# One transformer block on one core: transfers beside the weights issued by rank and spaced apart, gets in four parts

## The chip, the core and the metric

The kernel runs on one core of a Trainium2 chip. The metric is the device time of one execution in microseconds (us). Three runs of the kernel before took 3470.78 to 3471.49 us, median 3471.28 us. One more execution was recorded by the hardware profiler; all views below are of that one.

## What is computed

The input `x` has 8 sequences of 1024 rows of 512 numbers, `cond` one row of 512 per sequence; everything is float32. Per sequence (cut to what matters):

```python
mod = silu(condition) @ Wada + bada
sh_a, sc_a, gt_a, sh_m, sc_m, gt_m = split(mod, 6, axis=1)
xm = layernorm(x, g1, be1) * (1 + sc_a) + sh_a
x  = x + gt_a * attention(xm, Wqkv, Wproj, bproj)   # causal, 16 heads of 32
xm = layernorm(x, g2, be2) * (1 + sc_m) + sh_m
x  = x + gt_m * (gelu(xm @ W1 + b1) @ W2 + b2)      # W1 512x2048
```

## The kernel before

**Tiling.** The 8 x 1024 rows are cut into 16 blocks of 512 (`blocks`, numbered `n`, two per sequence). Each 512x512x512 product is done by a Strassen-like scheme of seven products of 256x256x256 (`strassen`); such a product is 32 matmul records of the profile, and its weights are one piece `w` of 256 KB. Sums of weight quarters are made once and kept in HBM (`kept_up_S`, `kept_down_S`, `kept_qkv_S`, `kept_proj_S`).

**Order of the work.** The program is one straight list of instructions for each engine, written by a planner inside the kernel. It keeps an estimated clock per engine (`now`), the time at which each value will be there (`written`), and two streams on TensorE: attention (`attend`), and the linear steps listed by window in `plan` (line 277 to 313). Of several threads it takes the one whose operands are due first (`work`, `step_aside`). A value whose transfer has not been issued stands at `NEVER`. In window `w`, with `n = w - 1`, from the third window on the steps are: the last "up" steps of block `n - 1`; the load of the residual rows of block `n` (`load_xr`); `v` of block `w`; the output projection of `n` (`proj`); its second normalization (`mt`); the "down" steps of `n - 1`; `q` and `k` of block `w + 1`; the first "up" steps of `n`, among them the load of the rows of a later block (`load_xa`).

**Transfers.** Nearly all are issued by SyncE (queue SP), in the order in which the planner emits them, and each waits there for what it needs:
- Weight pieces go through a ring of 9 buffers (`fetch`, line 380): a piece is fetched when the one nine places ahead has been used. Each fetch moves `queue_free`, the planner's idea of the queue, on by 450 ns.
- Rows of `x` for the first normalization (`load_x`, line 426, into the one buffer `hat`) and residual rows (`load_xr`, line 1442, into `xr`) are four transfers of 256 KB each, emitted together on the spot.
- From block 4 on for the first normalization (key `a`) and from block 3 to 13 for the second (key `m`), rows are turned by way of HBM instead of on TensorE (`turn_rows`, line 758): DVE transposes 32x32 squares, four puts of 256 KB (line 776) write them to `turned`, and one get of 1 MB (line 782) reads them back as `xm`. Then `modulated` scales each of the four column blocks `c` of `xm` (line 841 or 847). The first "up" product needs `c` = 0 and 1 only; the operands of most later ones need all four.
- Results are stored per half block (`store`, line 1266): two transfers of 256 KB at once.
- Puts, gets and stores stand in the list `transfers`; `run_transfers` (line 630) emits the one with the earliest ready time once `queue_free` and that time have passed, and moves `queue_free` on by 700 ns. A get becomes ready 7000 ns after the last put. `run_transfers(True)` empties the list at once; `stored_by` calls it when a buffer is to be reused whose stores are not yet emitted.
- Rows of the gates are broadcast from HBM (`gate_broadcasts`, line 595), two of 256 KB for the attention gate, on the spot; for even `n` this stands right before `load_xr`.

Of the kernel before, what the change touches and what calls it, by code (L numbers as in the profile page):

```python
# [22 lines left out]
def kernel(  # L23
# [261 lines left out]
    for w in range(1, NB):  # L285
        n = w - 1
        m = mlp_steps(n)
        even = blocks[n][1] == 0
        rows_a = [("rows", blocks[n][0], "a")] if even else []
        rows_m = [("rows", blocks[n][0], "m")] if even else []  # L290
        at = [("at", w + 2)] if w + 2 < NB else []
        ups = m[:1] + ([("load_xa", w + 2)] if w + 2 < NB else []) + m[1:3]
        ups += ([("norm_a", w + 2)] if w + 2 < NB else []) + m[3:4] + at
        head = rows_a + [("load_xr", n)]
        if w == 1:
            steps = head + [("k", w + 1), ("proj", n), ("mt", n), ("q", w + 1)]
# [12 lines left out]
        if w == NB - 1:  # L309
            plan[w] += late + downs[:2]  # L310
            downs = downs[2:]
# [111 lines left out]
    def row_tile(name):  # L423
        return tmp.tile([P, NTT, D], F32, tag="hat", name=name, bufs=1)

    def load_x(n):
        b, h = blocks[n]
        rows = row_tile(f"hat_{n}")
        if is_turned(f"a{n}"):
            for a in range(P // SQ):  # L430
                r0 = h * TB + a * P
                nc.sync.dma_start(
                    rows[a * SQ : (a + 1) * SQ, :, :],
                    x[b, r0 : r0 + P, :].rearrange("(t r) d -> r t d", r=SQ),
                )
        else:
            for t in range(NTT):
                nc.sync.dma_start(rows[:, t, :], x[b, h * TB + t * P : h * TB + (t + 1) * P, :])
        return [rows[:, t, :] for t in range(NTT)]

    x_pre = {0: load_x(0)}
    ada = {}
    for i in (1, 0):
        ada[i] = act.tile([P, NC, TB], F32, tag="hT", name=f"ada_{i}", bufs=NQ)
# [180 lines left out]
                return  # L625
            jobs.pop(i)[0]()

    transfers = []

    def run_transfers(everything=False):  # L630
        while transfers:
            i = min(range(len(transfers)), key=lambda i: transfers[i][0])
            if not everything and max(queue_free[0], transfers[i][0]) > now["PE"]:
                return
            ready, transfer = transfers.pop(i)
            queue_free[0] = max(queue_free[0], now["PE"], ready) + 700
            transfer()

    pool_jobs = []
# [33 lines left out]
    def normalize(tiles, key, sources):  # L673

        for t in range(NTT):
            written["hat", key, t] = NEVER
        mv = small.tile([P, NTT, 2], F32, tag="mv", name=f"mv_{key}")
        rstd = small.tile([P, NTT], F32, tag="rstd", name=f"rstd_{key}")
        offset = small.tile([P, NTT], F32, tag="offset", name=f"offset_{key}")
        got = []  # L680

        def statistics(t):
            st = small.tile([P, nc.vector.BN_STATS_DIM], F32, tag="st", name=f"st_{key}_{t}")
# [64 lines left out]
    def turn_first():  # L748
# [6 lines left out]
                note_pe(TR, "whole", [("hat", "a0", t)], ["st"])  # L755
        first_turned.append(st)

    def turn_rows(key, tiles, xm):

        squares = xm.rearrange("p c (j r) -> p (c j) r", r=P)  # L760
# [2 lines left out]
        def turn(t):  # L763
# [4 lines left out]
            if t == NTT - 1:  # L768
                ready = now["DVE"] + SYNC
                for a in range(P // SQ):  # L770
                    transfers.append((ready, lambda a=a: put(a)))

        def put(a):
            if a == P // SQ - 1:
                transfers.append((queue_free[0] + 7000, get))
            nc.sync.dma_start(
                there[:, ts(a, P)].rearrange("(k r) n -> r k n", r=SQ),
                squares[a * SQ : (a + 1) * SQ, :, :],
            )

        def get():
            nc.sync.dma_start(xm, there.rearrange("(c p) n -> p c n", p=P))
            written["spread", key] = queue_free[0] + 5000

        written["spread", key] = NEVER
        for t in range(NTT):
            add_job(lambda t=t: turn(t), [("hat", key, t)], key)

    def modulated(key, gain, shift, b, guards):
# [26 lines left out]
        turned = first_turned.pop() if key == "a0" else None  # L816
        if rows_turned:
            turn_rows(key, got, xm)
            yield [("spread", key)], []
        for c in range(NC):  # L820
            if rows_turned:
                if c:
                    yield [("spread", key)], []
                from_ps, held = xm[:, c, :], ("spread", key)
            elif turned is None:
                if c:
                    yield [("hat", key, 0)], [BANK]
# [308 lines left out]
    def project_half(n):  # L1136
# [3 lines left out]
        for other in ("B11", "B21", "B22"):  # L1140
            written[f"p{n}", other] = written["att", n]
        for t in range(NTT):
            xt_job = lambda t=t: add_to(
                residual[n][:, t, :], gate_rows["gba"], [("row", "gba")], [("xr", n, t)]
            )
            pool_jobs.append((xt_job, [("xr", n, t)]))
# [1 line left out]
        def put(f, t, bank, ps, other, reads, last):  # L1148
# [7 lines left out]
            else:  # L1156
                combine_out(y, bank, ps, other, reads, [ky], last=last)
                add_to(y, gate, [("row", "ga")], [ky], ALU.mult)
            add_to(residual[n][:, half(t, 2), c], y, [ky], [("xr", n, 2 * t), ("xr", n, 2 * t + 1)])

        def done():
            run_pool_jobs(True)
            normalize([residual[n][:, t, :] for t in range(NTT)], f"m{n}", [("xr", n, t) for t in range(NTT)])
            written["normal", n] = 0.0
# [4 lines left out]
    def project_out(n):  # L1169
# [2 lines left out]
        attT = qTs[n]  # L1172
        tiles = [residual[n][:, t, :] for t in range(NTT)]
        for t, xt in enumerate(tiles):
            xt_job = lambda t=t, xt=xt: add_to(xt, gate_rows["gba"], [("row", "gba")], [("xr", n, t)])
            pool_jobs.append((xt_job, [("xr", n, t)]))
        last = n == NB - 1
        begun = []
# [87 lines left out]
    def store(n, t):  # L1266
# [4 lines left out]
        unstored.append(n)  # L1271

        def move():
            unstored.remove(n)
            for i in (2 * t, 2 * t + 1):
                nc.sync.dma_start(rows[i], residual[n][:, i, :])

        transfers.append((ready + 1000, move))

    def stored_by(n):  # L1280
        while n in unstored:
# [136 lines left out]
    def perform(step):  # L1418
# [7 lines left out]
        elif kind == "gates":  # L1426
            yield from gates(step[1])
        elif kind == "load_xa":
            x_pre[step[1]] = load_x(step[1])
            written["x", f"a{step[1]}"] = now["PE"] + 6000  # L1430
        elif kind == "load_xr":
            n = step[1]
            b, h = blocks[n]
# [5 lines left out]
            else:  # L1439
                xr = xrp.tile([P, NTT, D], F32, tag="xr", name=f"xr_{n}")  # L1440
            residual[n] = xr
            for t, rows in enumerate(row_tiles_of(x[b, h * TB : (h + 1) * TB, :], n)):
                nc.sync.dma_start(xr[:, t, :], rows)
# [652 lines left out]
```

## Time and profile before

| | |
|---|---|
| median of 3 runs | 3471.28 us |
| the profiled execution | 3470.92 us |
| its span, first to last instruction | 3469.2 us |
| TensorE weight load, busy | 1778.0 us (51%) |
| VectorE busy | 2055.4 us (59%) |
| ScalarE busy | 1301.4 us (38%) |
| GpSimd busy | 1944.2 us (56%) |
| moved by DMA | 489.91 MB, mean 141 GB/s |

The engines are PE (TensorE), PEld (its weight loads), DVE (VectorE), ACT (ScalarE), POOL (GpSimd) and SP (SyncE, which issues transfers). A row of the list of waits reads: engine, line, what it waited for: total us, times, longest. A row of the timeline reads: start, length, engine, line, operation, out<-in, count, and in brackets how long the engine had been idle and what ended that. A piece of the chain of waits reads: start, length, what. A row of the table by stage reads: stretch, length, then busy us (and instructions) of PE, PEld, DVE, ACT and POOL, the granted TensorE clock, the busy share of the DMA engines, and GB/s.

### The profile page before, as it was taken

The numbers are of one execution on the slowest core, as the hardware profiler recorded it, in microseconds if no ns is written. First come the engines' busy times: TensorE is split into PE (matmuls) and PEld (weight loads), VectorE is DVE, ScalarE is ACT, GpSimd is POOL, SyncE is SP. The second block draws the span as 40 slices with busy tenths as digits, with TensorE's granted clock in tenths as the row PEclk, the third lists the DMA queues.
The fourth block names the chain that finished last, engine by engine and source line by source line (L and its number), as shares of the span: only waits on it lengthen the run. The fifth ranks groups of instructions, "written<-read, shape, count | busy, mean of one in ns | idle before, by whom it ended". The sixth has DMA issues, their size and how long they took to land.

```text
span 3469.2 us, 122474 instructions
## 1 busy us (share of the span) xinstructions
PE 3423.4 (99%) x55442; PEld 1778.0 (51%) x55442; DVE 2055.4 (59%) x2262; ACT 1301.4 (38%) x1444; POOL 1944.2 (56%) x2101
## 2 busy tenths in 40 slices
PE   8999999999999999999999999999999999999999
PEld 5544554555545554455554555454554545544555
DVE  6765666646565465664756547575466745656364
ACT  2345244343343433434333353443524334242421
POOL 3766757656267471774626755277553774446530
PEclk9999999999999999999999999999999999999999
DMA  6833434345544454444544445444464454633444
GB/s 226 277 127 87 120 108 138 109 117 159 156 141 134 127 152 146 138 136 128 167 135 144 136 132 175 127 140 135 133 187 121 129 150 121 187 115 88 120 143 136
DMA packets 378508, 489.91 MB, mean 141 GB/s; under 512 B 27284, under 2 KB 234444, under 8 KB 377988
## 3 DMA queue, kind: packets, MB, share of 16 engines
q1 hardware_dynamic: 377792, 481.79, 47.1%
q8 instruction: 437, 7.16, 0.9%
q14 instruction: 83, 0.68, 0.1%
q10 hardware_dynamic: 196, 0.28, 0.0%
HBM read 428.44 MB, written 53.53 MB: 139 GB/s over the span
## 4 chain that ended last, share of the span: by engine, by line
PE 89%; DVE 4%; DMA 4%; ACT 1%; issue 1%; POOL 1%; SPq 0%; DVEq 0%; ACTq 0%; POOLq 0%
PE bank L233 62%; PE sc L1692 8%; PE po L1826 7%; PE st L1785 7%; PE st L1773 3%; DVE mx L1709 2%; DMA w<-kept_proj_S 2%; PE bank L1847 2%; DMA w<-in_L_cond_Wproj_dram 1%; DVE sc L1706 1%; ACT pT L1798 1%; DMA xm_m<-turned_m 1%; PE bank L1747 0%; DVE hT L1299 0%; DMA xr<-in_x_dram 0%
## 5 line engine op out<-in xcount | busy, mean ns | idle before, releaser
L1911 POOL TENSOR_TENSOR pT<-pT,pT 128x256 f32<-128x256 f32 (+3 forms) x1254 | 1213.5, 1003 | 143.1 <-ACT pT L1798 112.3
L1798 ACT ACTIVATE pT<-st 128x2048 f32<-128x2048 f32 x288 | 541.1, 1879 | 1075.2 <-PE st L1785 989.3
L233 PE MATMUL bank<-w,hT 128*32 128x256 f32 x14336 | 814.1, 380 | 0.0
L1709 DVE TENSOR_REDUCE mx<-sc 128x4 f32<-128x2048 f32 (+3 forms) x384 | 665.7, 1754 | 215.3 <-PE sc L1692 209.2
L233 PEld LDWEIGHTS bank<-w,hT 128*32 128x32 f32 x14336 | 454.5, 110 | 357.6 <-issue 74.7
L233 PE MATMUL bank<-xm_m,w 128*32 128x256 f32 x8192 | 500.7, 381 | 4.6 <-DVE xm_m L841 4.5
L1803 POOL TENSOR_SCALAR_AFFINE_SELECT pT<-pT 128x512 f32<-128x512 f32 x256 | 177.1, 710 | 436.8 <-ACT pT L1798 431.5
L233 PE MATMUL bank<-t_m,w 128*32 128x256 f32 x6144 | 384.2, 381 | 0.1
L233 PEld LDWEIGHTS bank<-xm_m,w 128*32 128x32 f32 x8192 | 257.2, 110 | 228.7 <-issue 65.1
L1692 PE MATMUL sc<-kT,qT 32*128 32x512 f32 (+3 forms) x3072 | 329.3, 520 | 2.9 <-DVE mx L1709 1.8
L1706 DVE TENSOR_TENSOR sc<-sc,mask 128x1024 f32<-128x1024 f32 (+1 forms) x160 | 162.8, 1017 | 242.9 <-PE sc L1692 167.2
L1826 PE MATMUL po<-pT,v 128*32 128x512 f32 (+3 forms) x3072 | 304.9, 491 | 0.0
L1785 PE MATMUL st<-qT,kT 32*128 32x512 f32 (+3 forms) x3072 | 300.1, 486 | 0.0
L233 PEld LDWEIGHTS bank<-t_m,w 128*32 128x32 f32 x6144 | 190.2, 110 | 178.4 <-issue 51.7
L233 PE MATMUL bank<-xm_a,w 128*32 128x256 f32 x3968 | 239.3, 380 | 2.4 <-ACT xm_a L847 1.1
L190 POOL TENSOR_TENSOR qT<-top,rec 128x512 f32<-128x512 f32 x60 | 78.5, 1309 | 276.1 <-ACT rec L1865 276.1
L222 DVE TENSOR_TENSOR hT<-bank,u_u 128x512 f32<-128x512 f32 x192 | 130.0, 686 | 153.2 <-PE bank L233 150.7
L1692 PEld LDWEIGHTS sc<-kT,qT 32*128 32x128 f32 x3072 | 129.7, 184 | 161.5 <-issue 54.7
L233 PE MATMUL bank<-w,qT 128*32 128x256 f32 (+1 forms) x2944 | 191.6, 399 | 3.2 <-DMA w<-in_L_cond_Wproj_dram 3.2
L233 PE MATMUL bank<-t_a,w 128*32 128x256 f32 x2944 | 181.7, 380 | 0.0
L233 PEld LDWEIGHTS bank<-xm_a,w 128*32 128x32 f32 x3968 | 127.7, 110 | 97.4 <-issue 13.9
L1230 ACT ACTIVATE hT<-hT,cols 128x512 f32<-128x512 f32 x256 | 164.2, 711 | 27.2 <-DVE hT L222 26.5
(240 smaller groups left out, 3418.2 us busy)
## 6 DMA issues: line engine op xcount, KB each, us to landing
w<-in_L_cond_W_dram SPq DMA_DIRECT2D x384, 256.0 KB
w<-kept_up_S SPq DMA_DIRECT2D x256, 256.0 KB
w<-kept_down_S SPq DMA_DIRECT2D x256, 256.0 KB
w<-kept_qkv_S SPq DMA_DIRECT2D x180, 256.0 KB
w<-in_L_cond_Wqkv_dram SPq DMA_DIRECT2D x147, 256.0 KB
hat<-in_x_dram SPq DMA_DIRECT2D x64, 256.0 KB
xr<-in_x_dram SPq DMA_DIRECT2D x64, 256.0 KB
out_dram<-xr SPq DMA_DIRECT2D x64, 256.0 KB
```

Of the source, the lines that this page charges most:

```text
L222: nc.vector.tensor_tensor(out, src, other, op)
L233: nc.tensor.matmul(ps[r], columns, rhs, start=start, stop=stop, skip_group_check=True)
L1230: nc.scalar.activation(hT[:, i, :], hT[:, i, :], AF.Gelu, bias=cols[:, O_B1 + f : O_B1 + f + 1])
L1692: nc.tensor.matmul(sc[:, j, c0 : c0 + w], qTs[n][r, gg, ts(qt, P)], keys_of(n, kh)[r, gg, :w], start=True, stop=True, skip_group_check=True,)
L1706: nc.vector.tensor_tensor(place, place, shape_of.to_broadcast(place.shape), ALU.add)
L1709: nc.vector.tensor_reduce(maxima[n, gg][:, kh, qt, :], sc[:, :, c0 : c0 + w], axis=AX.X, op=ALU.max)
L1773: nc.tensor.matmul(st[:, j, c0 : c0 + w], minus_ones[r, :], row[r, TB - w :], start=(c0 == 0), stop=False, skip_group_check=True,)
L1785: nc.tensor.matmul(st[:, j, c0 : c0 + w], kT[r, gg, ts(k % NTT, P)], qT[r, gg, TB - w :], start=False, stop=True, skip_group_check=True,)
L1798: nc.scalar.activation(pT[:, :, :used], st[:, :, :used], AF.Exp, scale=scale)
L1803: nc.gpsimd.affine_select(diagonal, diagonal, pattern=[[0, HPG], [1, P]], compare_op=ALU.is_ge, fill=0.0, base=0, channel_multiplier=-1,)
L1826: nc.tensor.matmul(po[r, TB - w :], v[:, k % NTT, g * P + j * hd : g * P + (j + 1) * hd], pT[:, j, c0 : c0 + w], start=(k == 0), stop=last ...
L1911: nc.gpsimd.tensor_tensor(into, into, pT[:, j, c0 : c0 + w], ALU.add)
```

## The change

Every transfer but a weight, a kept sum and a gate row now goes through `transfers` with a rank: PATH (puts and gets) before LOAD (rows) before STORE. Of those that are ready, the lowest rank goes first, and each moves `queue_free` on by 1700 ns. Rows are loaded in four entries of their own, a store is two entries, and the get is four of 256 KB, one per `c`, each with its own time of arrival. Before a use of rows whose load has not been emitted, `arrived` empties the list. The assumed times of arrival change. The attention gate's rows of the next sequence move from before `load_xr` of an even block to the end of the window before, ahead of the first "up" step.

```diff
-        rows_a = [("rows", blocks[n][0], "a")] if even else []
+        rows_a = [("rows", blocks[n][0], "a")] if n == 0 else []
...
-        plan[w] = steps + rows_m + ups[:i]
+        rows_a = [("rows", blocks[w][0], "a")] if not even else []
+        plan[w] = steps + rows_m + rows_a + ups[:i]
...
-    transfers = []
+    transfers, coming = [], []
+
+    PATH, LOAD, STORE = range(3)
+    SPACE = 1700
...
         while transfers:
-            i = min(range(len(transfers)), key=lambda i: transfers[i][0])
-            if not everything and max(queue_free[0], transfers[i][0]) > now["PE"]:
+            due_now = [i for i, (ready, *_) in enumerate(transfers) if ready <= now["PE"]]
+            if everything:
+                i = min(range(len(transfers)), key=lambda i: transfers[i][0])
+            elif queue_free[0] > now["PE"] or not due_now:
                 return
-            ready, transfer = transfers.pop(i)
-            queue_free[0] = max(queue_free[0], now["PE"], ready) + 700
+            else:
+                i = min(due_now, key=lambda i: transfers[i][1::-1])
+            ready, _, transfer = transfers.pop(i)
+            queue_free[0] = max(queue_free[0], now["PE"], ready) + SPACE
             transfer()
...
+    LANDED = 5500
...
         def put(a):
             if a == P // SQ - 1:
-                transfers.append((queue_free[0] + 7000, get))
+                for c in range(NC):
+                    transfers.append((queue_free[0] + LANDED, PATH, lambda c=c: get(c)))
...
-        def get():
-            nc.sync.dma_start(xm, there.rearrange("(c p) n -> p c n", p=P))
-            written["spread", key] = queue_free[0] + 5000
-
-        written["spread", key] = NEVER
+        def get(c):
+            nc.sync.dma_start(xm[:, c, :], there[ts(c, P), :])
+            written["spread", key, c] = queue_free[0] + 3000
+
+        for c in range(NC):
+            written["spread", key, c] = NEVER
...
+    def arrived(what):
+        while what in coming:
+            run_transfers(True)
+
...
-    LANDING = 10000
+    LANDING = 6000
...
-        transfers.append((ready + 1000, move))
+        for i in (2 * t, 2 * t + 1):
+            unstored.append(n)
+            transfers.append((ready + 1000, STORE, lambda i=i: move(i)))
...
-            x_pre[step[1]] = load_x(step[1])
-            written["x", f"a{step[1]}"] = now["PE"] + 6000
+            def later(load):
+                coming.append(key)
+                transfers.append((now["PE"], LOAD, lambda: landing(load)))
+
+            def landing(load):
+                load()
+                coming.remove(key)
+                written[key] = NEVER if key in coming else queue_free[0] + 4000
...
+            def load(t, rows):
+                coming.remove(("xr", n))
+                nc.sync.dma_start(xr[:, t, :], rows)
+                written["xr", n, t] = max(now["PE"], stored.get(n - 1, 0.0), queue_free[0]) + LANDING
+
             for t, rows in enumerate(row_tiles_of(x[b, h * TB : (h + 1) * TB, :], n)):
-                nc.sync.dma_start(xr[:, t, :], rows)
-                landed = max(now["PE"], stored.get(n - 1, 0.0)) + LANDING + 700 * t
-                written["xr", n, t] = landed
+                written["xr", n, t] = NEVER
+                coming.append(("xr", n))
+                transfers.append((now["PE"], LOAD, lambda t=t, rows=rows: load(t, rows)))
```

More of the change, by code (lines that the diff above doesn't have):

```diff
@@ L424, in row_tile, with load_x @@
         return tmp.tile([P, NTT, D], F32, tag="hat", name=name, bufs=1)
-    def load_x(n):
+    def load_x(n, later):
         b, h = blocks[n]
         rows = row_tile(f"hat_{n}")
+        pairs = []
         if is_turned(f"a{n}"):
@@ L431, in load_x @@
                 r0 = h * TB + a * P
[L432 to L435, printed above, removed]
+                from_x = x[b, r0 : r0 + P, :].rearrange("(t r) d -> r t d", r=SQ)
+                pairs.append((rows[a * SQ : (a + 1) * SQ, :, :], from_x))
         else:
             for t in range(NTT):
-                nc.sync.dma_start(rows[:, t, :], x[b, h * TB + t * P : h * TB + (t + 1) * P, :])
+                r0 = h * TB + t * P
+                pairs.append((rows[:, t, :], x[b, r0 : r0 + P, :]))
+        for to, from_x in pairs:
+            later(lambda to=to, from_x=from_x: nc.sync.dma_start(to, from_x))
         return [rows[:, t, :] for t in range(NTT)]
-    x_pre = {0: load_x(0)}
+    x_pre = {0: load_x(0, lambda load: load())}
     ada = {}
@@ L682, in statistics @@
         def statistics(t):
+            arrived(("x", key))
             st = small.tile([P, nc.vector.BN_STATS_DIM], F32, tag="st", name=f"st_{key}_{t}")
@@ L770, in turn @@
                 for a in range(P // SQ):
-                    transfers.append((ready, lambda a=a: put(a)))
+                    transfers.append((ready, PATH, lambda a=a: put(a)))
         def put(a):
             if a == P // SQ - 1:
-                transfers.append((queue_free[0] + 7000, get))
+                for c in range(NC):
+                    transfers.append((queue_free[0] + LANDED, PATH, lambda c=c: get(c)))
             nc.sync.dma_start(
@@ L822, in modulated @@
                 if c:
[L823 to L824 removed]
+                    yield [("spread", key, c)], []
+                from_ps, held = xm[:, c, :], ("spread", key, c)
             elif turned is None:
@@ L1158, in put @@
                 add_to(y, gate, [("row", "ga")], [ky], ALU.mult)
+            arrived(("xr", n))
             add_to(residual[n][:, half(t, 2), c], y, [ky], [("xr", n, 2 * t), ("xr", n, 2 * t + 1)])
         def done():
+            arrived(("xr", n))
             run_pool_jobs(True)
@@ L1174, in project_out @@
         for t, xt in enumerate(tiles):
-            xt_job = lambda t=t, xt=xt: add_to(xt, gate_rows["gba"], [("row", "gba")], [("xr", n, t)])
+            xt_job = lambda t=t, xt=xt: arrived(("xr", n)) or add_to(xt, gate_rows["gba"], [("row", "gba")], [("xr", n, t)])
             pool_jobs.append((xt_job, [("xr", n, t)]))
@@ L1270, in store, with move @@
         stored[n + 1] = max(stored.get(n + 1, 0.0), ready)
-        unstored.append(n)
-        def move():
+        def move(i):
             unstored.remove(n)
-            for i in (2 * t, 2 * t + 1):
-                nc.sync.dma_start(rows[i], residual[n][:, i, :])
-        transfers.append((ready + 1000, move))
+            nc.sync.dma_start(rows[i], residual[n][:, i, :])
+        for i in (2 * t, 2 * t + 1):
+            unstored.append(n)
+            transfers.append((ready + 1000, STORE, lambda i=i: move(i)))
     def stored_by(n):
@@ L1428, in perform @@
         elif kind == "load_xa":
-            x_pre[step[1]] = load_x(step[1])
-            written["x", f"a{step[1]}"] = now["PE"] + 6000
+            key = ("x", f"a{step[1]}")
+            def later(load):
[5 more added lines that the diff above has]
+                written[key] = NEVER if key in coming else queue_free[0] + 4000
+            written[key] = NEVER
+            x_pre[step[1]] = load_x(step[1], later)
         elif kind == "load_xr":
```

4 lines of the change are left out of this document (2 added, 2 removed).

## The prediction, made before the changed kernel had run

> **What bounds the kernel now.** I read the page's first part first, for the share of each engine, and then the list of what TensorE waited for, which says how much a change of transfers could give at all.
>
> ```profile
> span 3469.2 us, 122474 instructions
> ...
> PE 3423.4 (99%) x55442; PEld 1778.0 (51%) x55442; DVE 2055.4 (59%) x2262; ACT 1301.4 (38%) x1444; POOL 1944.2 (56%) x2101
> ```
>
> PE is busy for all but 3469.2 - 3423.4 = 45.8 us. The change leaves every matmul in place, so whatever it gains has to come out of these 45.8 us, apart from matmuls that ran slowly. The list of waits of PE over the whole span names the pieces:
>
> ```profile
> PE st L1773 <- DVE mx L1709: 7.5, 12, 1.9
> PE bank L1747 <- POOL mcols L1731: 5.9, 7, 1.6
> PE bank L520 <- DMA ada<-in_L_cond_Wada_dram: 5.3, 1, 5.3
> PE bank L233 <- DVE xm_m L841: 4.5, 1, 4.5
> ...
> PE bank L233 <- DMA w<-in_L_cond_Wproj_dram: 3.2, 2, 1.6
> PE bank L233 <- DMA w<-kept_proj_S: 2.3, 4, 0.8
> ```
>
> The largest two, 13.4 us, are the softmax maxima on DVE and POOL, which the change does not touch. The 5.3 us are the first load of the program, also untouched. Within reach are three rows: 3.2 + 2.3 = **5.5 us** of waiting for weights of the output projection, six times, and **4.5 us** of one wait for the turned rows of a block.
>
> **Term 1: the weights of the projection.** The timeline of SP and the chain of waits show the longest of the six, at block 6:
>
> ```profile
> 1406.09 0.47 SPq L599 DMA_DIRECT2D row_ga<-kept_ga  x1
> 1406.61 0.42 SPq L599 DMA_DIRECT2D row_gba<-kept_gba  x1
> 1407.08 3.03 SPq L1443 DMA_DIRECT2D xr<-in_x_dram  x4
> 1410.21 4.48 SPq L390 DMA_DIRECT2D w<-in_L_cond_Wproj_dram  x2
> ```
>
> ```profile
> 1410.21 15.27 DMA w<-in_L_cond_Wproj_dram
> ```
>
> ```profile
> 1425.62 1.50 PE L233 MATMUL bank<-w,qT 128*32 128x256 f32 x24 [1.65 <-DMA w<-in_L_cond_Wproj_dram]
> ```
>
> Six transfers of 256 KB leave SP in 4 us, the first projection weight stands behind them, needs 15.27 us to land, and the matmul comes 1.65 us too early. How fast such a burst drains is seen at block 5, where POOL uses the residual rows tile by tile:
>
> ```profile
> 1202.27 2.53 SPq L1443 DMA_DIRECT2D xr<-in_x_dram  x4
> ```
>
> ```profile
> 1208.24 1.29 POOL L190 TENSOR_TENSOR xr<-xr,row_gba 128x512 f32<-128x512 f32 x1 [14.33 <-DMA xr<-in_x_dram]
> 1212.01 1.28 POOL L190 TENSOR_TENSOR xr<-xr,row_gba 128x512 f32<-128x512 f32 x1 [2.48 <-DMA xr<-in_x_dram]
> 1215.80 1.26 POOL L190 TENSOR_TENSOR xr<-xr,row_gba 128x512 f32<-128x512 f32 x1 [2.51 <-DMA xr<-in_x_dram]
> ```
>
> Beside the weights a tile lands every 3.8 us. When SP has issued four in 2.53 us, about 4 - 2.53/3.8 = 3.3 stand ahead of the next weight. After the change they are emitted at least 1700 ns apart, and with a weight's 450 ns between them 2.15 us; when the fourth is out, 6.45 us have passed and 4 - 6.45/3.8 = 2.3 are left. So the worst weight has one tile less ahead of it, up to 3.8 us, against a longest wait of 1.65 us; at even blocks the two gate rows are gone from this place as well. I take all of **-5.5 us**. The other end is 0, should only the place of the burst move. The gate rows now stand ahead of the first up step, with no burst of rows behind them; I cost them at nothing, since weights there have the same nine-piece lead, and at 1.65 us each if that cover is gone.
>
> **Term 2: the turned rows of block 5.** SP's timeline, the chain, and PE's timeline:
>
> ```profile
> 1294.32 0.43 SPq L776 DMA_DIRECT2D turned_m<-xm_m  x1
> ...
> 1299.40 0.76 SPq L776 DMA_DIRECT2D turned_m<-xm_m  x1
> 1300.26 1.97 SPq L1276 DMA_DIRECT2D out_dram<-xr  x2
> ...
> 1304.55 2.15 SPq L1276 DMA_DIRECT2D out_dram<-xr  x2
> ...
> 1310.71 1.18 SPq L782 DMA_DIRECT2D xm_m<-turned_m  x1
> ```
>
> ```profile
> 1310.71 11.04 DMA xm_m<-turned_m
> ```
>
> ```profile
> 1316.04 1.91 PE L233 MATMUL bank<-t_a,w 128*32 128x256 f32 x32
> 1322.43 3.51 PE L233 MATMUL bank<-xm_m,w 128*32 128x256 f32 x32 [4.48 <-DVE xm_m L841]
> 1326.15 1.93 PE L233 MATMUL bank<-xm_a,w 128*32 128x256 f32 x32 [0.21 <-DVE u_k L222]
> ```
>
> ```profile
> 1319.00:1324.00 5.00, 1.57 (x17) 0.94 (x21) 2.15 (x4) 0.82 (x1) 0.00 (x0) 0.86 0.59 215
> ```
>
> Four stores are issued right after the puts; the get follows 11.3 us after the last put and takes 11.04 us. PE idles 4.48 us, and the granted clock of that stretch is 0.86: the product behind the gap takes 3.51 us where its like takes 1.91 us. So the wait costs 4.48 + 1.60 = 6.1 us, more than its row in the list. [...]
>
> After the change the first parts become ready 1700 + 5500 = 7.2 us after the last put was emitted, against 700 + 7000 = 7.7 us; the puts themselves, 1.7 us apart in the trace, come 2.15 us apart, so the last one up to 1.35 us later. The four parts start at least 1.7, more often 2.15 us apart: the last starts 5.1 to 6.45 us after the first. Part 1 thus starts 1.2 to 3.0 us later than the whole get would have, but lands without the other half ahead of it; half of 11.04 us is 5.5 us. The first up product needs parts 0 and 1 only: it gains 5.5 - 1.2 = 4.3 us at best and 2.5 us at worst. The other products need part 3, which starts 4.6 to 7.3 us later than the get did; its own quarter, 2.8 us, replaces 11.04 us, so it lands between 3.6 us earlier and 1.0 us later. The tail of `k` (two products, the first at 1326.15, some 3.5 us) stands ready to fill the space in between, which the planner now sees, since it knows each part's own arrival. I take **-4 us** out of 6.1. The ends: -6.1 if nothing is waited for any more, and +6 if the parts come as late as they are emitted and land no faster.
>
> Elsewhere the turned rows have time to spare; block 7, on SP, ACT and PE:
>
> ```profile
> 1724.59 0.39 SPq L782 DMA_DIRECT2D xm_m<-turned_m  x1
> ```
>
> ```profile
> 1730.32 2.93 ACT L847 ACTIVATE xm_m<-xm_m,shiftm,gainm 128x512 f32<-128x512 f32 x4 [16.60 <-DMA xm_m<-turned_m]
> ```
>
> ```profile
> 1756.20 1.94 PE L233 MATMUL bank<-xm_m,w 128*32 128x256 f32 x32
> ```
>
> They land 5.7 us after the get and are used 25.9 us after that. A chain 6 us longer is hidden there by the `q` and `k` products.
>
> **What costs nothing, and why.** Three more issues for each of the 23 gets (`a` of blocks 4 to 15, `m` of 3 to 13) are 69 x 0.39 us (the get of block 7, above) = 27 us of SP, which is far from the bound:
>
> ```profile
> SPq L392 <- PE bank L233: 1436.5, 682, 21.8
> ...
> SPq L390 <- DMA xr<-in_x_dram: 41.3, 18, 3.3
> ```
>
> SP waits 1436.5 us for PE to free weight buffers in one row alone. The 41.3 us, fetches held up behind bursts of rows, should shrink. Without that cover the 27 us would show in weights that land late. Rows and stores that come some us later are hidden as long as their users have the `v` step or more ahead of them; the residual rows' first use lies behind the seven products of `v`, 13 us at 1.91 us each, and four entries at 2.15 us take 8.6 us. Only in window 2 does the projection follow the load directly; there the list may be emptied once. Should `arrived` or `stored_by` empty the list, SP gets a burst like those of before, at the price that they have now, up to 1.65 us each. At the end of the program the issue order decides the last half microsecond:
>
> ```profile
> 3463.65 0.36 SPq L1356 DMA_DIRECT2D out_dram<-xr  x1
> 3464.06 1.37 SPq L1276 DMA_DIRECT2D out_dram<-xr  x2
> 3466.12 0.33 SPq L1356 DMA_DIRECT2D out_dram<-xr  x1
> ```
>
> If the second of the two L1276 stores slips behind the last L1356, the end comes some 0.5 us later: I take +0.3, between 0 and +0.5.
>
> The planner's new times also shift the interleaving of attention and linear work everywhere. The trace cannot show that order. I bound it by the softmax waits, 7.5 + 5.9 = 13.4 us: a third more or less of these is 4 us on either side, and I take 0.
>
> **Sum.** -5.5 - 4.0 + 0.3 = -9.2 us. The profiled execution took 3470.92 us (1.7 us around its span), 0.36 us under the median of the runs; from the median, 3471.28 - 9.2 = 3462.1, rounded to **3462.0 us** (-0.27%).
>
> **Rivals.**
> 1. *Only the projection's waits go; block 5 stays as it is.* For it: 1300 to 1311 is where stores, puts and get of one block crowd, and a list emptied by `stored_by` there would send them together again. Against it: the stores have lower rank. 3471.28 - 5.5 = 3465.8 us.
> 2. *It does not do what it says for PE.* Rows, weights and stores are as many bytes as before, a spaced burst still drains at one tile per 3.8 us, and 2.15 us is faster than that; if the weights land just as late, the 5.5 us stay, block 5 stays, and the new order gives or takes up to 4 us: 3471 us, between 3467 and 3475.
> 3. *Slower: the longer way of the turned rows becomes the wait at the first up step.* The last part is emitted up to 7.3 us later. Place: the first up products of the 11 blocks from 3 to 13. Price: where no slack is left, up to 7.3 us of idling plus 1.6 us of slow clock, 8.9 us for each block. It decides once two blocks lose it, 17.8 - 5.5 = +12.3 us: 3483.6 us. Against it stand 25.9 us of slack at block 7; for it, that block 5 had none, and that the new order may move others there. [...] No row here shows a turned get in parts; the weights of 256 KB are what the trace has, and there the queue keeps many in flight.
> 4. *More than the sum.* If POOL and DVE wait less for rows, part of the 13.4 us goes too: another 5 us, 3457 us.
>
> **Chances.** The forecast 0.42 (3459 to 3465), rival 1 0.21, rival 2 0.14, rival 3 0.16, rival 4 0.07. A difference under 0.2%, 6.9 us, is about what a measurement of this kernel can tell from no change; the bound is 3464.3 us below and 3478.2 us above. Faster by more: rival 4, and the forecast but for its upper edge, 0.07 + 0.42 = 0.49, and 0.02 of rival 1, makes 0.51. Slower by more: rival 3, 0.16. Within: the rest, 0.33. The range runs from 3457 us (rival 4's middle) to 3474 us (rival 2's upper part); outside are rival 3 and half of rival 4, 0.195 in all.
>
> **What would show it.** Term 1: no wait of PE for `kept_proj_S` or `Wproj` in the list of waits, four separate `xr` issues on SP, and under 15.27 us for that weight in the chain. Term 2: no gap of 4.48 us ahead of an up step, a granted clock of 1.00 in that stretch, and the four parts of the get landing one after the other. Wrong would be a new row of waits for `xm_m` or `xm_a` at several blocks, waits for weights elsewhere in the list, or a PE busy time that differs from 3423.4 us by more than 4 us, since then it is the order of the matmuls that decides.

## The result and the profile after

The kernel after took 3463.89 us, median of 14 runs (3462.82 to 3465.78); the kernel before, on the same chip, 3471.11 us, median of 14. The ratio is 0.998, 95% interval 0.9973 to 0.9987: **7.2 us or 0.21% faster**, between 4.5 and 9.4 us. The forecast was 3462.0 us.

The profiled execution of after took 3465.39 us, 1.5 us above that median. The first part of its page:

```profile
span 3463.7 us, 122539 instructions
...
PE 3424.3 (99%) x55442; PEld 1776.1 (51%) x55442; DVE 2069.1 (60%) x2295; ACT 1288.6 (37%) x1422; POOL 1940.4 (56%) x2090
```

TensorE is idle for 3463.7 - 3424.3 = 39.4 us, where it was 45.8: 6.4 us less. The list of its waits (engine, line, what it waited for: total us, times, longest):

```profile
PE st L1812 <- DVE mx L1748: 7.5, 12, 1.9
PE bank L1786 <- POOL mcols L1770: 5.9, 7, 1.6
...
PE sc L1731 <- DVE mx L1748: 3.0, 4, 2.0
```

No row of the list names `Wproj` or `kept_proj_S` any more: the 5.5 us of Term 1 are gone as waits. The row of 4.5 us for `xm_m` is gone too (0.4 us are left), but one has grown: score units wait for the softmax maximum 3.0 us, 2.0 of them at one place, where the list of before has

```profile
PE sc L1692 <- DVE mx L1709: 1.8, 5, 0.6
```

The two softmax rows that the forecast left untouched, 7.5 and 5.9 us, are the same to a tenth of a microsecond.

The table by stage says where. Of before (stretch, length, then busy us and instructions of PE, PEld, DVE, ACT and POOL, clock, DMA share, GB/s):

```profile
25.00:100.00 75.00, 72.77 (x1189) 42.06 (x1185) 55.41 (x72) 23.04 (x31) 27.67 (x36) 1.00 0.63 205
...
1300.00:1340.00 40.00, 35.31 (x576) 18.86 (x568) 16.84 (x21) 5.08 (x7) 2.48 (x2) 0.96 0.60 190
1340.00:2000.00 660.00, 655.17 (x10571) 334.96 (x10564) 401.62 (x428) 256.98 (x280) 392.60 (x417) 1.00 0.48 138
```

The same stretches of after:

```profile
25.00:100.00 75.00, 72.76 (x1157) 41.89 (x1152) 53.80 (x71) 22.94 (x31) 25.96 (x35) 0.98 0.62 199
...
1300.00:1340.00 40.00, 36.93 (x621) 19.72 (x616) 16.62 (x20) 8.40 (x12) 5.49 (x5) 1.00 0.68 205
1340.00:2000.00 660.00, 658.48 (x10636) 336.08 (x10632) 411.41 (x443) 252.97 (x272) 393.89 (x414) 1.00 0.48 139
```

Around block 5 (1300 to 1340) idling fell from 4.69 to 3.07 us and the clock rose to 1.00, and from 1340 to 2000 it fell from 4.83 to 1.52 us. The first row shows a trap: at equal busy time, after did 32 matmuls fewer at a clock of 0.98. From 24.90 to 28.20 us its clock was 0.50; that is about 1.7 us lost near the start. It belongs to this execution and not to the change: the profiled executions of e5 and e11 below, with the matmuls in the order of after, did 1187 and 1188 in that stretch at a clock of 1.00, and that of e8, in the order of before, 1160 at 0.98. The slow stretch near the start took the place of the slow product at block 5, so PE's busy time did not fall; it also fits that this execution lies above its median.

**The projection.** SP's timeline of after at block 6:

```profile
1403.43 0.60 SPq L1478 DMA_DIRECT2D xr<-in_x_dram  x1
1404.72 0.39 SPq L391 DMA_DIRECT2D w<-in_L_cond_Wproj_dram  x1
1405.16 0.59 SPq L1478 DMA_DIRECT2D xr<-in_x_dram  x1
```

The four `xr` loads alternate with the weights, and no gate rows stand ahead of them.

**Block 5.** SP, the chain of waits, and PE:

```profile
1305.87 0.60 SPq L1296 DMA_DIRECT2D out_dram<-xr  x1
1309.35 0.58 SPq L1296 DMA_DIRECT2D out_dram<-xr  x1
1311.11 1.16 SPq L1296 DMA_DIRECT2D out_dram<-xr  x2
1312.32 4.30 SPq L796 DMA_DIRECT2D xm_m<-turned_m  x4
```

```profile
1312.32 11.26 DMA xm_m<-turned_m
```

```profile
1320.75 1.91 PE L233 MATMUL bank<-t_a,w 128*32 128x256 f32 x32
1322.59 1.14 PE L1731 MATMUL sc<-kT,qT 32*128 32x512 f32 x8
1324.41 0.64 PE L233 MATMUL bank<-xm_m,w 128*32 128x256 f32 x8 [0.68 <-issue]
1325.42 1.50 PE L233 MATMUL bank<-xm_m,w 128*32 128x256 f32 x24 [0.37 <-DVE xm_m L856]
1328.95 1.14 PE L1731 MATMUL sc<-kT,qT 32*128 32x512 f32 x8 [2.03 <-DVE mx L1748]
```

The four parts did not go out apart from each other. `stored_by`, called for `k` of block 7, emptied the list: two stores and then all four parts at once. The first part landed 11.26 us after its issue, where the whole get of before had taken 11.04 us. What did change is PE's row: the tail of `k` and a score unit now stand *ahead* of the first up product. The waits are 0.68 + 0.37 + 2.03 = 3.1 us at full clock, in place of 4.48 + 0.21 us and a product slower by 1.60 us, 6.3 us together: **3.2 us less** in this execution.

The full clock there is not certain. A later profiled execution of the same kernel (after_again, with e9 below) has nearly the same waits, 0.90 + 0.37 + 2.02 us, and then a slow product:

```profile
1329.68 1.14 PE L1731 MATMUL sc<-kT,qT 32*128 32x512 f32 x8 [2.02 <-DVE mx L1748]
1330.75 3.44 PE L233 MATMUL bank<-t_m,w 128*32 128x256 f32 x32
```

It takes 3.44 us in place of 1.93, so with 0.2 us more of waiting about half of the 3.2 us is lost again in that execution.

### The profile page after: what moved, and what is told of

Same layout as the page of the kernel before. It is cut to its first block, busy times and chain, and to the rows that moved or that the text cites. A ratio compares the mean times of both kernels' runs of the same rounds, so it can differ in the third digit from the quotient of the medians.

```text
span 3463.7 us, 122539 instructions
## 1 busy us (share of the span) xinstructions
PE 3424.3 (99%) x55442; PEld 1776.1 (51%) x55442; DVE 2069.1 (60%) x2295; ACT 1288.6 (37%) x1422; POOL 1940.4 (56%) x2090
## 4 chain that ended last, share of the span: by engine, by line
PE 90%; DVE 4%; ACT 2%; DMA 2%; issue 1%; POOL 1%; SPq 0%; DVEq 0%; ACTq 0%; POOLq 0%
PE bank L233 62%; PE sc L1731 8%; PE po L1865 7%; PE st L1824 7%; PE st L1812 3%; DVE mx L1748 2%; PE bank L1886 2%; ACT pT L1837 1%; DMA w<-kept_up_S 1%; DVE sc L1745 1%; DMA xm_m<-turned_m 1%; PE bank L1786 1%; DVE hT L1321 0%; ACT hT L1252 0%; PE bank L847 0%
```

## The experiments

The question was which of the change's parts does this. Theory A: at block 5 it is the order of the matmuls, which the planner chose because its estimate of the arrival is a later one, and at the projection it is the burst that is gone. Theory B, the forecast's: the transfers themselves, by rank, spacing and parts, land sooner. Each kernel was timed beside the kernel before on the same chip; differences are against that.

**e1: the order alone.** In the kernel before, one number: the arrival that the planner assumes for the second rows of block 5.

```diff
-            written["spread", key] = queue_free[0] + 5000
+            written["spread", key] = queue_free[0] + 5000 + (4000 if key == "m5" else 0)
```

> The kernel before, with one number changed: the planner takes the get of block 5 to arrive 9000 ns after queue_free instead of 5000. Every transfer is as before; on TensorE only the order around the first up step of block 5 changes, the two products that end k of block 7 and one unit of scores now stand ahead of it. Theory A (term 2 came from the order of the matmuls, not from how the transfers go): the gap of 4.48 us before the first up product and its slow product go, some 3 us of new waits remain as in the changed kernel, and the time falls by 2 to 4 us, to about 3468.0 us; the six waits for projection weights, 5.5 us, stay. Theory B (term 2 came from the get in parts landing earlier): the turned rows land as late as before, the order alone gains nothing, 3470 to 3472 us.

Measured: 3465.54 us against 3470.51, ratio 0.9984 (0.9976 to 0.9993), -5.0 us. PE at block 5, and the chain there:

```profile
1320.29 1.14 PE L1692 MATMUL sc<-kT,qT 32*128 32x512 f32 x8
1321.44 1.93 PE L233 MATMUL bank<-xm_m,w 128*32 128x256 f32 x32
1324.90 1.93 PE L233 MATMUL bank<-t_m,w 128*32 128x256 f32 x32 [1.53 <-DVE kT L222]
```

```profile
1309.67 10.89 DMA xm_m<-turned_m
```

The whole get still takes 10.89 us and follows the stores as before, but the product that uses it no longer waits. Theory A holds for block 5; the gain is above the 2 to 4 us that it gave, with an interval from 2.4 to 8.3 us. The projection's waits stayed, as they should in this kernel:

```profile
PE bank L233 <- DMA w<-in_L_cond_Wproj_dram: 3.0, 2, 1.5
...
PE bank L233 <- DMA w<-kept_proj_S: 1.3, 2, 0.7
```

**e8: the spaced loads alone.** In the kernel before, the four `xr` loads become entries of `transfers`, 1700 ns apart; the order of the matmuls is that of before.

```diff
+            def load(t, rows):
+                queue_free[0] += 1000
                 nc.sync.dma_start(xr[:, t, :], rows)
+
+            for t, rows in enumerate(row_tiles_of(x[b, h * TB : (h + 1) * TB, :], n)):
+                transfers.append((now["PE"], lambda t=t, rows=rows: load(t, rows)))
```

> The kernel before, with only the four residual loads put into the list of transfers, each moving queue_free on by 1700 ns; the matmuls keep their order exactly. Theory A (the projection's weights waited behind the burst): the waits for kept_proj_S and Wproj fall from 5.5 us to under 1 us, and the time to 3465.5 to 3467.5 us. Theory B (the burst drains no faster when it is spaced, the waits went because the gate rows moved or because the order changed): the waits stay at 3 us or more, 3469 to 3471 us.

Measured: 3468.28 us against 3470.51, ratio 0.9993 (0.9984 to 1.0001), -2.2 us, not certain by itself. The interval reaches from 5.6 us faster to 0.3 us slower. The list of PE's waits has no projection weight any more; it has the wait of block 5 (`xm_m`, 4.6 us), a row that was 0.8 us in before (`pT`), and a new one (`p_proj`):

```profile
PE sc L1697 <- ACT pT L1803: 2.5, 1, 2.5
...
PE bank L233 <- DVE p_proj L214: 1.3, 3, 0.5
```

All 5.5 us of waits for weights went, and 1.3 us came for `p_proj`: at the projection PE now waits for DVE to copy a result out of its bank. The profile of before has no such row, and in that of e2, with the burst, it is at most 0.2 us; every one without the burst has it, with 0.5 to 1.8 us. The longer wait for `pT` is less certain: the profiled execution is the longest of the eleven (3472.79 us), and in two executions of e9, below, that wait is absent and 1.4 us.

**e2: the burst put back.** In the kernel after, the `xr` loads are emitted together on the spot again; the order of the matmuls is that of after.

```diff
-                written["xr", n, t] = NEVER
-                coming.append(("xr", n))
-                transfers.append((now["PE"], LOAD, lambda t=t, rows=rows: load(t, rows)))
+                nc.sync.dma_start(xr[:, t, :], rows)
+                landed = max(now["PE"], stored.get(n - 1, 0.0)) + 10000 + 700 * t
+                written["xr", n, t] = landed
```

> The changed kernel, with the four residual loads issued together on the spot as before, and their planned arrivals as before; the matmuls keep the order of the changed kernel. Theory A: four or five waits for projection weights come back, 2.5 to 5 us in all, 3466.5 to 3469 us; the wait at block 6 stays small, because its gate rows are gone. Theory B: no difference, 3463 to 3465 us.

Measured: 3467.66 us against 3470.51, ratio 0.9989 (0.998 to 0.9998), -2.8 us. The waits for weights of the projection are back, 3.6 us:

```profile
PE bank L233 <- DMA w<-kept_proj_S: 2.2, 3, 1.5
...
PE bank L233 <- DMA w<-in_L_cond_Wproj_dram: 1.4, 1, 1.4
```

A row of 1.9 us for weights of the up step (`kept_up_S`) stands there too, but it is no mark of the burst: after_again, without the burst, has 1.9 us as well.

**e5: the gate rows put back** ahead of `load_xr` of even blocks, in the kernel after; the order of the matmuls is that of after.

```diff
-        rows_a = [("rows", blocks[n][0], "a")] if n == 0 else []
+        rows_a = [("rows", blocks[n][0], "a")] if even else []
...
-        plan[w] = steps + rows_m + rows_a + ups[:i]
+        plan[w] = steps + rows_m + ups[:i]
```

> The changed kernel, with the gate rows of the attention back ahead of the residual loads of even blocks; the matmuls keep the order of the changed kernel. Theory A (the burst of residual rows was the cause, the two gate rows only at block 6): a wait for a projection weight of at most 1.6 us comes back, 3464 to 3466 us. Theory B (the gate rows were the cause): 3 us or more come back, 3467 us or more.

Measured: 3464.37 us against 3470.51, ratio 0.9985 (0.9976 to 0.9994), -6.1 us, about what after itself gained, and the list of waits names no weight of the projection. Moving the gate rows shows no gain clear of the noise. On this chip e2 lies 3.3 us above e5; with e8 that puts the burst at 2 to 3 us by the medians.

**e9: both small edits in the kernel before**, e1 and e8 together, without ranks, parts, single stores or moved gate rows.

> The kernel before with the edits of e1 and e8 together: the later arrival planned for one get, and the four residual loads spaced. No ranks, no get in parts, no moved gate rows, stores in pairs. Theory A (the whole gain is these two, some 5 us from the order at block 5 and 2 to 4 us from the projection's weights): 7 to 9 us under the kernel before on the same chip, as good as the changed kernel or 1 us better, since e1's new wait at block 5 was 1.5 us. Theory B (ranks, parts or stores one by one have a share of their own): only 4 to 6 us under.

Measured: 3463.46 us against 3471.79, ratio 0.9978 (0.9968 to 0.9988), -8.3 us. Run once more beside the changed kernel itself:

> e9 once more, beside the changed kernel on the same chip. Theory A: within 1.5 us of the changed kernel, 7 to 9 us under the kernel before. Theory B (e9's lead was that of its chip): 2 us or more slower than the changed kernel.

> The changed kernel as it is, on the chip of the others. Both theories: 6 to 8 us under the kernel before.

Measured: e9 3463.30 us, ratio 0.9977 (0.9968 to 0.9986), -8.0 us; the changed kernel 3463.56 us, ratio 0.9979 (0.997 to 0.9987), -7.7 us, both against 3471.26 us. Within the noise, the two small edits give all of the gain. The two by themselves add up to 5.0 + 2.2 = 7.2 us.

**e3: the whole get.** In the kernel after, one get of 1 MB, with one arrival for all four parts.

```diff
-                for c in range(NC):
-                    transfers.append((queue_free[0] + LANDED, PATH, lambda c=c: get(c)))
+                transfers.append((queue_free[0] + LANDED, PATH, get))
...
+        def get():
+            nc.sync.dma_start(xm, there.rearrange("(c p) n -> p c n", p=P))
+            for c in range(NC):
+                written["spread", key, c] = queue_free[0] + 5000
```

> The changed kernel with the get as one transfer of 1 MB again, all four columns planned to arrive 5000 ns after queue_free. Theory A (the parts bring nothing by landing earlier; what they change is the planner's idea of arrivals): at block 5 a wait of 2 to 5 us as the planner's order has it, nothing elsewhere but waits that the planner itself puts in where it takes turned rows of even blocks for late: 2 to 10 us over the changed kernel. Theory B (a part lands well before a whole get): the first up product of block 5 and the first q and k products of even blocks wait 3 us or more each for turned rows in the list of waits, 10 us or more over the changed kernel.

Measured: 3478.18 us against 3471.79, ratio 1.0018 (1.0009 to 1.0027), +6.4 us. The waits that grew are those of another order:

```profile
PE st L1812 <- DVE mx L1748: 13.0, 18, 1.9
...
PE bank L233 <- ACT p_k L217: 3.5, 5, 0.7
```

Softmax maxima went from 7.5 to 13.0 us, at six places more, and `p_k` from 0.7 to 3.5 us. This is some 14 us over the changed kernel, the size that theory B had named, but its sign is missing: PE's waits for turned rows of key `m` sum to 2.9 us in the whole run, not to 3 us or more at each place. So this run does not price the parts: it changed the assumed arrivals too, and with them the order of the work.

**e7: only the stores that are needed.** In the kernel after, `stored_by` emits the stores of its own block and leaves the rest of the list.

```diff
         while n in unstored:
-            run_transfers(True)
+            first = min((e for e in transfers if of_block.get(id(e), (None,))[0] == n), key=lambda e: e[0])
+            transfers.remove(first)
+            queue_free[0] = max(queue_free[0], now["PE"], first[0]) + SPACE
+            first[2]()
```

> The changed kernel, except that stored_by emits only the stores of the block it needs, not the whole list. At block 5 the four parts of the get are then emitted 2 to 3 us apart, after the stores, instead of together; elsewhere only the same stores as before are emitted early. Theory A (a part issued alone lands in 5 us or less, the 11 us were the burst): parts land 4 to 6 us after their issue; the first part is issued some 6 us later than in the changed kernel, so it is there at about the same time, and the last one 3 to 5 us later: 0 to 4 us slower. Theory B (a get takes some 11 us whatever stands beside it, since the puts have to land first): the wait at block 5 grows by 5 us or more, 5 to 8 us slower.

Measured: 3474.73 us against 3471.79, ratio 1.0009 (1.0 to 1.0018), +2.9 us. SP and PE at block 5:

```profile
1317.54 0.59 SPq L796 DMA_DIRECT2D xm_m<-turned_m  x1
...
1325.09 0.32 SPq L796 DMA_DIRECT2D xm_m<-turned_m  x1
```

```profile
1327.91 1.08 PE L233 MATMUL bank<-xm_m,w 128*32 128x256 f32 x8 [3.45 <-issue]
1330.44 3.10 PE L233 MATMUL bank<-xm_m,w 128*32 128x256 f32 x24 [1.45 <-DMA xm_m<-turned_m]
...
1337.55 0.40 PE L1818 MATMUL st<-mrow,minus_ones 32*128 32x512 bf16 x4 [2.42 <-DVE mx L1754]
```

Here the parts do go out apart from each other, and the first one leaves 5.2 us later than in after. PE waits 3.45 + 1.45 + 2.42 us and 24 matmuls take 3.10 us where after needs 1.50. Sent alone, the first part still needed 9.7 us until DVE used it (at 1327.26, for 0.55 us), not the 4 to 6 us of theory A. The product starts 0.1 us after DVE was done with that part, as it does in after; but the profile names no engine and no transfer for the 3.45 us, so their cause is not shown. The whole run is some 11 us over the changed kernel, more than either theory gave; the order of the matmuls differs in places, and the rest stays open. The emptied list had put stores ahead of the parts, but it had also sent the parts in time.

**e4: less space.** In the kernel after, `SPACE = 700` in place of 1700.

> The changed kernel with SPACE at 700 instead of 1700. Theory A (what helps the projection is that a weight stands between two loads, which the ring gives at any spacing under 1.7 us): no waits for projection weights come back, the time within 2 us of the changed kernel apart from order, 5 to 8 us under the kernel before. Theory B (the bandwidth beside the weights is the limit, so the wider spacing is what helps): waits for projection weights of 2 us or more in all come back, 2 to 4 us under the kernel before.

Measured: 3519.04 us against 3471.79, ratio 1.0141 (1.0126 to 1.0157), **+47 us**. No theory foresaw that. The longest of the waits of PE, and that of DVE:

```profile
PE bank L233 <- DVE u_k L222: 18.0, 8, 6.5
```

```profile
DVE xm_m L856 <- DMA xm_m<-turned_m: 60.5, 18, 11.4
```

Not one row is a wait for a weight: the queue is not the trouble. DVE stands 60.5 us before turned rows that have not landed (17.3 us in after). The sums of `q` and `k` stand behind that in its list, and PE waits for those, 18.0 us for `u_k` and 8.1 us for `qT`. PE's timeline at block 5 has the largest case:

```profile
1318.27 3.64 PE L233 MATMUL bank<-xm_a,w 128*32 128x256 f32 x64
1328.38 3.64 PE L233 MATMUL bank<-t_a,w 128*32 128x256 f32 x32 [6.47 <-DVE u_k L222]
```

After 6.47 us of idling, 32 matmuls take as long as 64 took before. The suspect is the planner's estimate: `SPACE` also moves `queue_free` on, from which every arrival is worked out, so each part was assumed to be there sooner and DVE was told to use it sooner.

**e10: the same space, the arrivals of after.** e4, with the estimates put back by hand to what the wider spacing gave.

```diff
-    LANDED = 5500
+    LANDED = 6500
...
-            written["spread", key, c] = queue_free[0] + 3000
+            written["spread", key, c] = queue_free[0] + 4000 + 1000 * c
...
-    LANDING = 6000
+    LANDING = 7000
```

(and later arrivals for the two kinds of row loads)

> The kernel e4, SPACE at 700, but with the planned arrivals moved back to where they stood at 1700: LANDED 6500, a part at 4000 + 1000 c, the loads at 8000 and 7000 + 1000 t behind queue_free. Theory A (e4 lost because the planner took the parts of the get for landed too early, and DVE, which works in order, stood before them while PE waited for what was queued behind): the waits of DVE for xm_m fall from 60.5 us to under 30 us, PE's for u_k and qT from 26 us to under 6 us, and the time is 0 to 5 us under the kernel before, on which the order it plans decides. Theory B (spacing on the queue is what matters, since 700 lets the transfers crowd): it stays 20 us or more over the kernel before.

Measured: 3468.53 us against 3471.26, ratio 0.9993 (0.9984 to 1.0002), -2.7 us. DVE's wait is back near the 17.3 us that it has in after:

```profile
DVE xm_m L856 <- DMA xm_m<-turned_m: 21.0, 7, 9.4
```

So nearly all of the 47 us was the estimate, not the traffic. Against the changed kernel on this chip 5.0 us remain. The order of the matmuls differs in places, with one wait of 4.5 us for `u_k`, so how much of the 5.0 us is the spacing itself stays open.

**e11: a wait for stores that nothing needs.** The keys of odd blocks have a buffer of their own, which residual rows never use; for them `stored_by` guards nothing. In the kernel after it is called for even blocks only.

```diff
         if tag == "kT":
-            stored_by(n - 3)
+            if n % 2 == 0:
+                stored_by(n - 3)
```

> The changed kernel, with stored_by left out ahead of the k of odd blocks, whose buffer no residual rows share; the matmuls keep the order of the changed kernel exactly. At block 5 the get's first part then goes ahead of the last two stores, and the parts are not emitted in one burst. Theory A (the get of block 5 took 11 us because of what the queue held ahead of it, stores among it): the first part lands 1 to 3 us earlier, the waits at block 5 fall from 3.1 us to under 1.5 us, and the time to 1 to 2 us under the changed kernel, 7.5 to 10 us under the kernel before. Theory B (it is not the stores): no difference, or 1 to 3 us slower, since the last parts are emitted 4 us later.

Measured: 3459.21 us (3458.19 to 3460.08) against 3471.26, ratio 0.9966 (0.9954 to 0.9979), **-12.0 us, faster than both kernels**, and 4.3 us under the changed kernel on the same chip. The order of the matmuls is exactly that of after. SP, the chain and PE at block 5:

```profile
1308.69 0.59 SPq L796 DMA_DIRECT2D xm_m<-turned_m  x1
...
1321.14 0.55 SPq L1297 DMA_DIRECT2D out_dram<-xr  x1
```

```profile
1308.69 8.70 DMA xm_m<-turned_m
```

```profile
1318.67 1.93 PE L233 MATMUL bank<-xm_a,w 128*32 128x256 f32 x32 [1.92 <-DVE u_k L222]
...
1326.01 1.14 PE L1732 MATMUL sc<-kT,qT 32*128 32x512 f32 x8 [0.55 <-DVE mx L1749]
```

Now the first part leaves 3.6 us sooner, two of the stores wait until after the parts, and it lands in 8.70 us: this is what the forecast had described. But PE's waits at block 5 are still 1.92 + 0.55 = 2.5 us, only 0.6 us less than in after: DVE, idle for 5.08 us before it scaled the first part, held up `u_k`. So these waits explain little of the 4.3 us. The clock explains some: the profile of e11 has a clock of 1.00 from 25 to 100 us, where that of after has 0.98, about 1.7 us as above, and 1.00 from 1300 to 1340 us; that of after_again has the product of 3.44 us in place of 1.93, about 1.5 us, at block 5. For the rest, e11 did 9724 matmuls from 600 to 1200 us where after did 9704, 13083 against 13060 from 2000 to 2800 us, and 9700 against 9640 from 2800 to 3400 us, at a clock of 1.00 in both; what makes this difference stays open.

## Why the prediction was right, and where it was not

The time lay 1.9 us above the forecast and well inside its range; the reasons held only in part.

- **The bound.** Right: the gain came out of PE's idle time, 45.8 to 39.4 us, and the two softmax rows did not move.
- **Term 1, taken as -5.5 us.** The mechanism was right: the burst of rows ahead of the weights made the projection wait. e8 removes the waits by spacing alone, e2 brings 3.6 us of them back by the burst alone. The size was too large by the medians, 2.2 us (e8) and 3.3 us (e2 beside e5), though the interval of e8 still reaches 5.6 us. The step that failed, as far as this shows, is "I take all of" it: when the weights come in time, PE waits at the same place for `p_proj`, 1.3 us in e8 and 0.7 us in after, so a part of the wait stays. The gate rows, costed at nothing, show no cost clear of the noise (e5).
- **Term 2, taken as -4 us.** The size was near (3.2 us by the rows of one execution, half of that by those of another, 5.0 us in e1), but that is in part luck, since the main step failed. "Lands without the other half ahead of it" did not happen: 11.26 us against 11.04 us. Rival 1 had named why, "a list emptied by `stored_by` there would send them together again", and so they went. Rival 1 in turn was wrong that block 5 would stay as it is, because the second step held: the tail of `k` filled the space, since the planner's estimate had moved. e1 shows that this step alone is enough, without one changed transfer.
- **What costs nothing.** Right for SP: its wait in fetches behind rows fell from 41.3 us to the row below. The +0.3 us at the end did not come: the two L1296 stores still leave between the two of L1378.

```profile
SPq L391 <- DMA xr<-in_x_dram: 7.1, 7, 1.6
```

```profile
3458.29 0.36 SPq L1378 DMA_DIRECT2D out_dram<-xr  x1
3458.70 0.92 SPq L1296 DMA_DIRECT2D out_dram<-xr  x2
3460.76 0.33 SPq L1378 DMA_DIRECT2D out_dram<-xr  x1
```

- **The order of the matmuls, taken as 0 within 4 us either way.** Its effect elsewhere was small in after. As a bound it was far too narrow for what this planner can do: a change of its assumed arrivals gave +47 us in e4.
- **Rival 3**, turned rows that come too late for their users, did not occur in after. Its mechanism is real, as e4 shows (DVE waits 60.5 us for such rows), but the planned use moved there, more than the landing, and the time was lost through DVE's order and not in PE's own wait for the rows.

## What to carry to other kernels

Where a program orders its work by assumed arrival times, a change of the transfers is two changes, of the traffic and of the order: try each alone, and the order by a single changed estimate, before the traffic gets the credit. A wait that is removed is worth its row only if nothing else is late just behind it, so look for the next thing due at that place. A use that is planned too early stops an engine for everything behind it in its list: in e4 DVE stood 60.5 us before turned rows and the run was 47 us longer, where the burst in the queue cost 2 to 3 us. That speaks for estimates that err on the late side, though no run here prices one that is much too late.

## What was not expected of the hardware

The landing time of a transfer hardly followed its size. The 1 MB get of block 5 took 11.04 us (10.89 us in e1) and that of block 7 5.7 us; a first part of 256 KB took 11.26 us behind four stores (after), 8.70 us behind two (e11), and 9.7 us until DVE used it when it was sent without the others (e7). That what else was moving, stores and weights, is the cause is a guess; no run isolates it.

The length of one gap did not decide whether the clock slowed. After 3.45 us of idling in e7, 8 matmuls took 1.08 us where after needs 0.64 us, and after 6.47 us in e4, 32 took 3.64 us in place of 1.91 us. But 2.10 us near the start of after were followed by two products of 2.41 and 3.24 us in place of 1.94, and 2.02 us at block 5 of after_again by the 3.44 us above, while 2.03 us at block 5 of after and 1.98 us near the start of before were followed by none.

Nor does PE's busy time in the 3.40 us before tell the two cases at block 5 apart. In after_again the product of 3.44 us lies in a stretch of 3.40 us with a clock of 0.50, and before it stands one in which PE was busy for 1.38 of 3.40 us:

```profile
1327.60:1331.00 3.40, 1.38 (x18) 0.48 (x18) 3.37 (x4) 0.58 (x1) 0.70 (x1) 1.00 0.94 253
1331.00:1334.40 3.40, 3.40 (x39) 1.72 (x35) 2.27 (x2) 0.00 (x0) 1.08 (x1) 0.50 0.32 116
```

The same work in after, 0.73 us earlier in its span, had PE busy for 1.37 of 3.40 us, and the clock after it was 1.00:

```profile
1326.87:1330.27 3.40, 1.37 (x18) 0.48 (x18) 3.37 (x4) 0.58 (x1) 0.70 (x1) 1.00 0.97 237
1330.27:1333.67 3.40, 3.40 (x68) 2.07 (x64) 3.37 (x3) 0.00 (x0) 1.09 (x1) 1.00 0.57 173
```

So the same gaps of about 2 us cost about 1.5 us of slow clock or nothing; what decides between the two was not shown.
